# The last step of the FP4 codes on ScalarE instead of VectorE, in a transformer block with FAVOR attention

## The chip, the core and the metric

The kernel runs on one core of a Trainium2 chip. A core has a matrix engine (TensorE, PE in the profile, with its weight loads shown as PEld), a vector engine (VectorE, DVE), an engine for activation functions (ScalarE, ACT), a general engine (GpSimd, POOL) and an engine that here only issues transfers (SyncE, SP). They run at the same time and wait for one another by semaphores. Each takes its own instructions strictly in order. Operands lie in on-chip memory of 128 partitions; PE writes to a separate accumulation memory of eight banks, from which DVE and ACT read.

The metric is the device time of one execution in microseconds. A profile is one execution in which the start and end of every instruction were recorded; its span runs from the first instruction to the last.

## The reference

The input is 16 sequences of 512 rows with 256 features. One block is computed: attention with positive random features, a layer norm, a gated feed-forward network with 4-bit weights and activations, and a second layer norm.

```
q, k = softmax of 16-element heads of (x Wq + bq), (x Wk + bk)
context = (q k^T / (sum q + EPS)) v          # no softmax over rows, so k^T v is summed first
x = layernorm(x + context Wo + bo)

def fp4_quant_dequant(x):                    # along the last dimension, blocks of 16
    scale = max(max|xb| / 6, 1e-12)
    xn = xb / scale
    q = _GRID[searchsorted(_MID, |xn|)] * sign(xn) * scale

gate, up = fq(x) fq(w_gate)^T, fq(x) fq(w_up)^T      # 256 -> 704
h = silu(gate) * up
x = layernorm(x + fq(h) fq(w_down)^T)                # 704 -> 256
```

Each value is rounded to one of 0, 0.5, 1, 1.5, 2, 3, 4, 6 times the scale of its block. What matters here is how the kernel rounds.

## The kernel before

The rows are worked in 32 pairs of 128-row tiles (two pairs to a sequence). For each sequence, `project` makes q and k (line 778, evicted by DVE at 781), `features` the exponentials (ACT, 801) and their sums and reciprocals (DVE, 803 and 814, multiplied by POOL at 820), and `key_values` the summed k^T v folded with Wo (PE 836, 852, 864; ACT copies `xk` at 843 and `M` at 870). For each pair, `attend` transposes q (PE 636, ACT copy `qT` at 639), multiplies (PE 892) and does the first layer norm; the result goes to device memory and comes back later. Then the feed-forward network, pair by pair: `quantise` makes the codes of x, `gate_up` multiplies (PE 957), applies Silu (ACT 962) and the product (DVE 964) and makes the codes of h, and `down` multiplies (PE 1026) and does the second norm (`norm`, DVE 733 or, for the last two pairs, 718 to 725).

The rounding to 4 bits is done in `codes` (line 642), once for each pair over 512 elements of x and twice over 704 elements of h:

1. DVE takes the maximum of each block of 16 (655), makes the scale and its reciprocal (659, 660) and multiplies (663).
2. ACT reads the upper 16 bits of each scaled float as an integer, multiplies it by `UNTIE` and adds `MAGIC_U` = 1.5 x 2^29 (666). At that size a float has steps of 64, so the addition rounds. The result `sq` is `MAGIC_U` plus a multiple of 64.
3. DVE reads the lower 16 bits of that float and shifts them left by six (668). What it writes is the code as a 16-bit float, ready to be used as BF16: into `xc` for x, into `hcs` for h.

The codes are then transposed. DVE transposes blocks of 32 x 32 (921 for x, 1002 for h), SP writes them to device memory and reads them back regrouped (676 and 681, in `regroup`), the scales go the same way (691, 699 and 704, in `spread_scales`), and POOL multiplies codes by scales (929 for x, 1009 for h). The last pair does not take this way: DVE multiplies its codes by the scales at once (`hd`, 977), PE transposes (991), and ACT and DVE copy (995).

The weights are rounded once at the start in `fp4_exact`, which has a shift of its own (582); the change doesn't touch it.

The order of the work is made by a planner when the program is built. Every step is recorded by `op` with its engine, an assumed duration, a due time and the buffers that it reads and writes. `Plan.order` (144) then places steps one at a time: on each engine, among the steps that could start earliest, the one with the earliest due time. The instructions are issued in that order, so a change of one step's engine or assumed duration can move all others. `port=True` marks DVE steps that the planner does not place beside a POOL step. Assumed durations come from `t_act`, `t_dve`, `t_ts` and `t_pool` (250 to 263). The seven accumulation banks that PE shares among its uses are handed out by the planner too (`Share`, 78).

Of the kernel before, what the change touches and what calls it, by code (L numbers as in the profile page):

```python
# [8 lines left out]
F32 = mybir.dt.float32  # L9
# [4 lines left out]
AF = mybir.ActivationFunctionType  # L14
ALU = mybir.AluOpType
AX = mybir.AxisListType

P = 128
# [25 lines left out]
MAGIC_U = 1.5 * 2.0**29  # L44
# [51 lines left out]
class Plan:  # L96
# [7 lines left out]
    def op(self, eng, us, due, fn, ins=(), outs=(), holds=(), table=None, port=None, name=""):  # L104
        o = Op()
        o.eng, o.us, o.fn, o.due, o.table, o.name = eng, us, fn, due, table, name

        o.port = eng == "POOL" if port is None else port
        o.preds, o.succs, o.new, o.bufs, o.end = set(), [], [], [], None
        ins = [x if isinstance(x, tuple) else (x, None) for x in ins]  # L110
        outs = [x if isinstance(x, tuple) else (x, None) for x in outs]
        for b, key in ins:
            for k, w in b.last.items():
                if key is None or k is None or k == key:
                    o.preds.add(w)
        for b, key in outs:
            if b not in o.new:
                o.new.append(b)
            for k, w in b.last.items():
                if key is None or k is None or k == key:  # L120
                    o.preds.add(w)
            for k, rs in b.reads.items():
                if key is None or k is None or k == key:
                    o.preds.update(rs)
        for b, key in ins:
            b.reads.setdefault(key, []).append(o)
        for b, key in outs:
            b.last[key] = o
            b.reads[key] = []
        for b in holds:  # L130
            if b not in o.new:
                o.new.append(b)
        for b in {id(b): b for b in [b for b, _ in ins + outs] + list(holds)}.values():
            b.users += 1
            o.bufs.append(b)
        o.preds.discard(o)
        for p in o.preds:
            p.succs.append(o)
        o.left = len(o.preds)
        o.at = len(self.ops)  # L140
        self.ops.append(o)
        return o
# [107 lines left out]
def t_dve(n):  # L250
    return 0.15 + n / 960.0


def t_act(n):
    return 0.16 + n / 1200.0


def t_ts(n):
    return 0.15 + n / 1920.0
# [7 lines left out]
def tile_favor_fp4_block(  # L267
# [16 lines left out]
    nc = tc.nc  # L284
# [23 lines left out]
    const = ctx.enter_context(tc.tile_pool(name="const", bufs=1))  # L308
# [9 lines left out]
    op = plan.op  # L318
# [48 lines left out]
    def bcast(ap, n):  # L367

        return ap.unsqueeze(2).to_broadcast([ap.shape[0], ap.shape[1], n])
# [5 lines left out]
    def upper(ap):  # L375

        return ap.bitcast(U16).rearrange("p (n t) -> p n t", t=2)[:, :, 1]

    def lower(ap):

        return ap.bitcast(U16).rearrange("p (n t) -> p n t", t=2)[:, :, 0]
# [30 lines left out]
    b_o = const.tile([P, D], F32, name="b_o")  # L412
    ident = const.tile([P, P], F32, name="ident")
    neg_half = const.tile([P, 2], F32, name="neg_half")
    magic = const.tile([P, 4], F32, name="magic")

    mask = const.tile([P, P // HD, HD], F32, name="mask")
    mask2 = mask.rearrange("p g d -> p (g d)")
# [58 lines left out]
    def fill():  # L477
        make_identity(nc, ident)
        nc.gpsimd.memset(neg_half, -0.5)
        nc.gpsimd.memset(nsh, 0.0)  # L480
        nc.gpsimd.memset(hcs, 0.0)
        nc.gpsimd.memset(magic[:, 0:1], MAGIC / 2.0)
        nc.gpsimd.memset(magic[:, 1:2], -MAGIC / 2.0)
        nc.gpsimd.memset(magic[:, 2:3], MAGIC_U)
        nc.gpsimd.memset(magic[:, 3:4], 31.5 * 2.0**-65)
        nc.gpsimd.memset(mask, 1.0)
        nc.gpsimd.affine_select(
            out=mask, in_=mask, compare_op=ALU.is_ge, fill=0.0,
            base=0, pattern=[[-HD, P // HD], [0, HD]], channel_multiplier=1,
        )  # L490
        nc.gpsimd.affine_select(
            out=mask, in_=mask, compare_op=ALU.is_ge, fill=0.0,
            base=HD - 1, pattern=[[HD, P // HD], [0, HD]], channel_multiplier=-1,
        )
# [147 lines left out]
    def codes(src, xn, sq, dst, key, n, scales, at, name, due, sat=None):  # L642

        (src, src_b), (xn, xn_b), (sq, sq_b) = src, xn, sq
        amax, nscale, inv = scales
        nb = n // BLK
        g = slice(key * nb, key * nb + nb)
        gs = slice(sat, sat + nb) if sat is not None else g  # L650

        def b3(ap):
            return ap.rearrange("p (g e) -> p g e", e=BLK)

        op("DVE", t_dve(n), due, lambda: nc.vector.tensor_reduce(  # L655
            amax[:, g], b3(src()), AX.X, ALU.max, apply_absolute_value=True), ins=[src_b], outs=[(amax, key)])

        def scale():
            nc.vector.tensor_scalar(nscale[:, gs], amax[:, g], -UP / 6.0, -1e-12 * UP, ALU.mult, ALU.min)
            nc.vector.reciprocal(inv[:, g], nscale[:, gs])  # L660

        op("DVE", 0.27 + 0.0073 * nb, due, scale, ins=[(amax, key)], outs=[(nscale, key), (inv, key)])
        op("DVE", t_dve(n), due, lambda: nc.vector.scalar_tensor_tensor(  # L663
            b3(xn()), b3(src()), TIE * UP / BIG, bcast(inv[:, g], BLK), ALU.mult, ALU.mult),
           ins=[src_b, (inv, key)], outs=[xn_b], holds=[sq_b])
        op("ACT", t_act(n) + 0.14, due, lambda: nc.scalar.activation(  # L666
            sq(), upper(xn()), AF.Identity, bias=magic[:, 2:3], scale=UNTIE), ins=[xn_b], outs=[sq_b])
        op("DVE", t_ts(n), due, lambda: nc.vector.tensor_scalar(
            dst[:, at : at + n], lower(sq()), 6, None, ALU.logical_shift_left), ins=[sq_b],
           outs=[(dst, key)], port=True)  # L670

    def regroup(src, dst, n, tag, name, due):

# [233 lines left out]
    def quantise(i, due):  # L907
        x1 = st[i]["x1"] = buf([2, D], "x1", X1, f"x1_{i}")
        d = st[i]["d"]
        dma(f"rx1_{i}", 3.5, due - PAIR, lambda: nc.sync.dma_start(x1.tile, d.tile), ins=[d], outs=[x1])  # L910
        n = 2 * D
        G = n // P
        flat = lambda b: b.tile.rearrange("p u d -> p (u d)")
        am, iv = (small(n // BLK, t + "x", f"{t}_x{i}") for t in ("am", "iv"))
        scales = am, buf([n // BLK], "nsx", 2, f"ns_x{i}"), iv
        xn, sq = (buf([2, D], "xq", 2, f"{t}_{i}") for t in ("xn", "sqx"))
        xc = buf([n], "xc", 2, f"xc_{i}", U16)
        codes((lambda: flat(x1), x1), (lambda: flat(xn), xn), (lambda: flat(sq), sq), xc, 0, n, scales, 0,
              f"x{i}", due)
        xw, xcT = (buf([4, 2 * 32], t, 2, f"{t}_{i}", U32) for t in ("xw", "xcT"))  # L920
        op("DVE", 0.15 + n / 2 / 960.0, due, lambda: nc.vector.transpose(
            xw.tile.rearrange("p q (u t) -> p q u t", u=2),
            xc.tile.bitcast(U32).rearrange("p (u q t) -> p q u t", u=2, q=4)), ins=[xc], outs=[xw], port=True)
        regroup(xw, xcT, 2 * 32, "x", f"x{i}", due)
        xs_ = buf([2 * P], "xs", 2, f"xs_{i}")
        xqT = buf([2 * DC, P], "xqT", 2, f"xqT_{i}")
        spread_scales(scales[1], 1, (lambda: xs_.tile, xs_), "x", f"x{i}", due, [xqT])
        for u in range(2):
            op("POOL", t_pool(D), due, lambda u=u: nc.gpsimd.tensor_tensor(  # L929
                xqT[:, DC * u : DC * (u + 1), :].rearrange("p c (a t) -> p c a t", t=32),  # L930
                xcT.tile.bitcast(BF16).rearrange("p a (u t c) -> p u c a t", u=2, c=2)[:, u],
                xs_[:, u * P : (u + 1) * P].rearrange("p (a t) -> p a t", t=32).unsqueeze(1).to_broadcast([P, DC, 4, 32]),
                ALU.mult,
            ), ins=[xcT, xs_], outs=[(xqT, u)])
        st[i]["xqT"] = xqT
# [134 lines left out]
    with tc.manual_schedule():  # L1070
        load_all()
        fill()
        for o in plan.order():
            for b in o.new:
                b.make()
            o.fn()
# [41 lines left out]
```

## Time and profile before

| | us |
|---|---|
| median of three runs | 791.95 (791.62 to 792.87) |
| the profiled execution, its own time | 793.69 |
| its span | 792.0 |
| PE busy | 768.6 (97%) |
| DVE busy | 656.7 (83%) |
| ACT busy | 416.5 (53%) |
| POOL busy | 455.9 (58%) |
| shift, 704 elements (line 668, 64 times) | 40.0, mean 0.627 |
| shift, 512 elements (line 668, 32 times) | 18.2, mean 0.569 |
| rounding on ACT, 704 elements (line 666, 64 times) | 56.2, mean 0.878 |
| rounding on ACT, 512 elements (line 666, 32 times) | 23.1, mean 0.721 |

A row of groups reads: line, engine, operation, what it writes and reads, shape, count, busy time, mean duration of one in ns, and the idle time of the engine just before such instructions with what ended it. A matmul with 32-bit operands goes through PE in two passes, which the profile counts as two instructions. In a row of a timeline, the first number is the start in microseconds from the start of the span, the second the length; a bracket gives the idle time before and the releaser. The granted clock is the share of full speed that PE was given.

### The profile page before, as it was taken

The numbers are of one execution on the slowest core, as the hardware profiler recorded it, in microseconds if no ns is written. First come the engines' busy times: TensorE is split into PE (matmuls) and PEld (weight loads), VectorE is DVE, ScalarE is ACT, GpSimd is POOL, SyncE is SP. The second block draws the span as 40 slices with busy tenths as digits, with TensorE's granted clock in tenths as the row PEclk, the third lists the DMA queues.
The fourth block names the chain that finished last, engine by engine and source line by source line (L and its number), as shares of the span: only waits on it lengthen the run. The fifth ranks groups of instructions, "written<-read, shape, count | busy, mean of one in ns | idle before, by whom it ended". The sixth has DMA issues, their size and how long they took to land.

```text
span 792.0 us, 10915 instructions
## 1 busy us (share of the span) xinstructions
PE 768.6 (97%) x3118; PEld 552.5 (70%) x3118; DVE 656.7 (83%) x1340; ACT 416.5 (53%) x893; POOL 455.9 (58%) x602
## 2 busy tenths in 40 slices
PE   7999999989998999999999999999999999999996
PEld 3567657657676777767777777777777777777774
DVE  2998999999888798697697798888878988778784
ACT  2347766868887783544545444444334444344441
POOL 5668788889887755574554435434533543543633
PEclk9999999999999999999999999999999999999998
DMA  9112411211111044404335454554554554464441
GB/s 277 45 55 86 142 53 54 82 60 62 54 53 62 30 129 133 118 37 124 100 112 138 145 171 136 152 149 134 149 154 135 145 149 140 125 179 129 136 130 41
DMA packets 104348, 89.23 MB, mean 113 GB/s; under 512 B 44512, under 2 KB 87904, under 8 KB 104288
## 3 DMA queue, kind: packets, MB, share of 16 engines
q1 hardware_dynamic: 90704, 71.49, 31.8%
q10 hardware_dynamic: 13584, 17.04, 6.0%
q8 instruction: 25, 0.41, 0.2%
q14 instruction: 35, 0.29, 0.1%
HBM read 53.28 MB, written 35.21 MB: 112 GB/s over the span
## 4 chain that ended last, share of the span: by engine, by line
PE 62%; DVE 12%; DMA 8%; POOL 8%; issue 4%; ACT 4%; SPq 2%; ACTq 0%; POOLq 0%; DVEq 0%
PE bank L957 26%; PE bank L1026 14%; PE bank L778 8%; PE bank L892 5%; PE bank L836 5%; POOL hq L1009 3%; DMA out_dram<-y 3%; DVE qk L781 2%; PE bank L636 2%; DVE mx L786 2%; DMA hcT<-g_h 2%; SPq L681 1%; POOL xqT L929 1%; DVE fs L803 1%; PE bank L852 1%
## 5 line engine op out<-in xcount | busy, mean ns | idle before, releaser
L957 PE MATMUL bank<-w_guT,xqT 128*128 128x352 f32 x1024 | 311.3, 459 | 0.0
L957 PEld LDWEIGHTS bank<-w_guT,xqT 128*128 128x128 f32 x1024 | 193.8, 190 | 100.4 <-ACT g L962 0.2
L1009 POOL TENSOR_TENSOR hq<-hcT,hq 128x384 f32<-128x384 bf16 x124 | 127.3, 1058 | 179.3 <-DMA hcT<-g_h 101.4
L1026 PE MATMUL bank<-w_dT,hq 128*128 128x256 f32 (+1 forms) x768 | 173.1, 379 | 1.1 <-DVE r L718 1.1
L1026 PEld LDWEIGHTS bank<-w_dT,hq 128*128 128x128 f32 (+1 forms) x768 | 144.9, 190 | 27.5 <-issue 1.9
L778 PE MATMUL bank<-w_qkv,xT 128*128 128x512 f32 x256 | 120.8, 602 | 3.8 <-DVE qk L781 1.9
L964 DVE TENSOR_TENSOR h<-bank,g 128x352 f32<-128x352 f32 x128 | 65.7, 515 | 50.9 <-ACT g L962 24.1
L962 ACT ACTIVATE g<-bank 128x352 f32<-128x352 f32 x128 | 57.6, 458 | 87.7 <-PE bank L957 77.8
L666 ACT ACTIVATE sq<-h,magic 128x704 f32<-128x704 uint16 x64 | 56.2, 878 | 79.2 <-DVE h L663 78.6
L820 POOL TENSOR_TENSOR qk<-qk,fr 128x512 f32<-128x512 f32 x64 | 67.0, 1073 | 20.5 <-DVE fr L814 18.9
L790 POOL TENSOR_TENSOR qk<-qk,mx 128x512 f32<-128x512 f32 x64 | 67.4, 1068 | 19.2 <-DVE mx L786 19.0
L778 PEld LDWEIGHTS bank<-w_qkv,xT 128*128 128x128 f32 x256 | 46.6, 193 | 45.4 <-issue 35.8
L755 ACT ACTIVATE y<-r,nb_d,rstd_d 128x256 f32<-128x256 f32 x60 | 32.6, 591 | 59.2 <-POOL nb_d L748 59.2
L929 POOL TENSOR_TENSOR xqT<-xcT,xs 128x256 f32<-128x256 bf16 x64 | 46.3, 740 | 27.6 <-DMA d_h<-sT_h 23.4
L836 PE MATMUL bank<-qk,x 128*128 128x256 f32 x256 | 59.7, 387 | 2.1 <-ACT qT L639 2.1
L892 PE MATMUL bank<-M,qT 128*128 128x256 f32 x256 | 59.6, 381 | 1.8 <-ACT M L870 1.8
L655 DVE TENSOR_REDUCE bank<-h 128x44 f32<-128x704 f32 x64 | 57.1, 893 | 1.6
L663 DVE SCALAR_TENSOR_TENSOR h<-h,bank 128x704 f32<-128x704 f32 x64 | 56.7, 886 | 2.1
L836 PEld LDWEIGHTS bank<-qk,x 128*128 128x128 f32 x256 | 49.5, 195 | 12.7 <-ACT qT L639 3.4
L781 DVE TENSOR_TENSOR qk<-bank,b_qkv 128x512 f32<-128x512 f32 x64 | 43.0, 681 | 18.3 <-PE bank L778 17.9
L892 PEld LDWEIGHTS bank<-M,qT 128*128 128x128 f32 x256 | 47.8, 190 | 13.2 <-ACT M L870 3.8
L885 POOL TENSOR_TENSOR xb<-x,b_o 128x512 f32<-128x512 f32 x32 | 41.0, 1285 | 22.8 <-DVE r L733 22.7
(137 smaller groups left out, 1083.3 us busy)
## 6 DMA issues: line engine op xcount, KB each, us to landing
g_h<-hw SPq DMA_DIRECT2D x31, 384.0 KB, 2.8
hcT<-g_h SPq DMA_DIRECT2D x124, 96.0 KB, 2.4
hq<-d_h SPq DMA_DIRECT2D x31, 384.0 KB, 4.1
dx<-x1n ACTq DMA_DIRECT2D x32, 256.0 KB, 2.0
x<-dx SPq DMA_DIRECT2D x32, 256.0 KB, 3.1
x<-_attn_hidden_states_dram SPq DMA_DIRECT2D x15, 512.0 KB, 3.5
out_dram<-y ACTq DMA_DIRECT2D x30, 256.0 KB, 3.3
xs<-d_x SPq DMA_DIRECT2D x32, 128.0 KB, 2.5
```

Source lines behind the costliest of these rows:

```text
L655: op("DVE", t_dve(n), due, lambda: nc.vector.tensor_reduce(amax[:, g], b3(src()), AX.X, ALU.max, apply_absolute_value=True), ins=[src_b], ...
L778: op("PE", t_pe(D2), due, lambda c=c, u=u, pqk=pqk: nc.tensor.matmul(pqk.tile, xT[:, 2 * c + u, :], w_qkv[:, c, :D2], start=c == 0, stop=c ...
L781: op("DVE", t_dve(D2), due, lambda t=t, pqk=pqk: nc.vector.tensor_tensor(qk[:, t, :], pqk.tile, b_qkv[:, :D2], ALU.add), ins=[pqk], outs=[ ...
L790: op("POOL", t_pool(D2), due, lambda g=g: nc.gpsimd.tensor_tensor(qk3()[:, g, :], qk3()[:, g, :], bcast(mx[:, g], HD), ALU.subtract), ins= ...
L820: nc.gpsimd.tensor_tensor(f3, f3, bcast(r[:, t * 2 * H : (t + 1) * 2 * H], HD), ALU.mult)
L836: nc.tensor.matmul(pxk[:, c * D : (c + 1) * D], x[:, t, c * P : (c + 1) * P], qk[:, t, D:], start=t == 0, stop=t == TPB - 1,)
L892: nc.tensor.matmul(pu(pa.tile)[:, u, :], qT[:, 2 * u + c, :], M[:, c, :], start=c == 0, stop=c == DC - 1,)
L957: op("PE", t_pe(F2), due + u * 0.2 * PAIR, lambda c=c, u=u, lo=lo, ps_=ps_: nc.tensor.matmul(ps_[:, :F2], xqT[:, 2 * u + c, :], w_guT[:, c ...
L962: op("ACT", t_act(F2), due, lambda g=g, pg=pg: nc.scalar.activation(g.tile, pg[:, :F2], AF.Silu), ins=[pg], outs=[g], table="silu")
L964: op("DVE", t_dve(F2), due, lambda g=g, h=h, pu_=pu_, k=k: nc.vector.tensor_tensor(h[:, k * F2 : (k + 1) * F2], pu_[:, :F2], g.tile, ALU.m ...
L1009: op("POOL", t_pool(TG * P), d, lambda u=u, c=c: nc.gpsimd.tensor_tensor(hq()[:, u, :, c, :].rearrange("p g (a t) -> p g a t", t=32), hcT. ...
L1026: op("PE", t_pe(D), due, lambda f=f, g=g, c=c, n=n, u=u: nc.tensor.matmul(pu(pd.tile)[:, u, :], hq()[:n, u, g, c, :], w_dT[:n, f, :], star ...
```

## The change

The third step of `codes` goes from DVE to ACT. Instead of shifting the lower 16 bits of `sq`, ACT subtracts `MAGIC_U` from the whole float and writes the difference, a multiple of 64 below 2^16, as a 16-bit integer. These are the same 16 bits. `magic` gets a fifth column that holds -`MAGIC_U` as the bias. The planner sees an ACT step with the assumed duration of the step before it, not a DVE step with `port=True`, and makes its order anew. From line 487 on, line numbers in the changed kernel are one higher, up to the removed line; from 672 on they are the same.

```diff
-    magic = const.tile([P, 4], F32, name="magic")
+    magic = const.tile([P, 5], F32, name="magic")
...
         nc.gpsimd.memset(magic[:, 3:4], 31.5 * 2.0**-65)
+        nc.gpsimd.memset(magic[:, 4:5], -MAGIC_U)
...
         op("ACT", t_act(n) + 0.14, due, lambda: nc.scalar.activation(
             sq(), upper(xn()), AF.Identity, bias=magic[:, 2:3], scale=UNTIE), ins=[xn_b], outs=[sq_b])
-        op("DVE", t_ts(n), due, lambda: nc.vector.tensor_scalar(
-            dst[:, at : at + n], lower(sq()), 6, None, ALU.logical_shift_left), ins=[sq_b],
-           outs=[(dst, key)], port=True)
+        op("ACT", t_act(n) + 0.14, due, lambda: nc.scalar.activation(
+            dst[:, at : at + n], sq(), AF.Identity, bias=magic[:, 4:5]), ins=[sq_b], outs=[(dst, key)])
```

## The prediction

> **What bounds the kernel now.** I read the page's first two parts, then the busy time by stretches, then PE's timeline where it stood idle, and last the end of the run.
>
> ```profile
> PE 768.6 (97%) x3118; PEld 552.5 (70%) x3118; DVE 656.7 (83%) x1340; ACT 416.5 (53%) x893; POOL 455.9 (58%) x602
> PEclk9999999999999999999999999999999999999998
> ```
>
> PE is busy 97% of the span, at full clock but for small dips. In the stretches (columns: window, length, busy us of PE, PEld, DVE, ACT, POOL with counts, clock, DMA share, GB/s) PE is without a gap from 260 to 770 us; what can be won lies before and behind.
>
> ```profile
> 93.00:260.00 167.00, 159.92 (x702) 112.91 (x702) 153.43 (x276) 124.89 (x271) 139.67 (x175) 0.99 0.17 57
> 260.00:420.00 160.00, 160.00 (x665) 117.64 (x665) 128.10 (x263) 89.56 (x188) 90.30 (x119) 1.00 0.34 102
> 420.00:770.00 350.00, 350.00 (x1344) 254.41 (x1344) 289.81 (x649) 152.25 (x340) 152.89 (x214) 1.00 0.51 145
> 770.00:792.00 22.00, 14.14 (x67) 11.03 (x65) 11.74 (x30) 4.34 (x10) 8.34 (x11) 0.91 0.11 37
> ```
>
> PE's timeline names what it waited for from 100 to 260 us, and at the end (bracket: idle before, releaser). Each row is a stop:
>
> ```profile
> 105.21 0.65 PE L636 MATMUL bank<-ident,x 128*128 128x128 f32 x4 [1.04 <-DVE wxm_g L580]
> 162.87 1.13 PE L778 MATMUL bank<-w_qkv,xT 128*128 128x512 f32 x2 [0.35 <-DVE qk L781]
> 169.53 1.98 PE L778 MATMUL bank<-w_qkv,xT 128*128 128x512 f32 x4 [0.78 <-DVE qk L781]
> 173.97 1.12 PE L778 MATMUL bank<-w_qkv,xT 128*128 128x512 f32 x2 [0.68 <-ACT xT L639]
> 189.25 1.13 PE L778 MATMUL bank<-w_qkv,xT 128*128 128x512 f32 x2 [0.78 <-DVE qk L781]
> 244.08 5.41 PE L836 MATMUL bank<-qk,x 128*128 128x256 f32 x16 [2.08 <-ACT qT L639]
> ...
> 771.49 0.93 PE L991 MATMUL bank<-ident,hd 128*128 128x128 f32 x6 [0.56 <-DVE hd L977]
> 774.24 0.96 PE L991 MATMUL bank<-ident,hd 128*128 128x128 f32 x6 [0.95 <-DVE hd L977]
> 778.84 6.72 PE L1026 MATMUL bank<-w_dT,hq 128*128 128x256 f32 x30 [0.61 <-DVE r L718]
> ```
>
> In the head DVE is at 92% (153.43 of 167 us) and releases most stops; the longest is ACT's. It costs twice, since the clock falls behind it:
>
> ```profile
> 244.00:250.00 6.00, 5.92 (x21) 4.91 (x22) 4.46 (x9) 5.28 (x10) 5.62 (x7) 0.72 0.14 53
> ```
>
> At 0.72 for 6 us PE loses 6 x 0.28 = 1.7 us.
>
> **The change, part by part.** The groups of the two steps that matter:
>
> ```profile
> L666 ACT ACTIVATE sq<-h,magic 128x704 f32<-128x704 uint16 x64 | 56.2, 878 | 79.2 <-DVE h L663 78.6
> L668 DVE TENSOR_SCALAR hcs<-sq 128x704 uint16<-128x704 uint16 x64 | 40.0, 627 | 2.8 <-ACT sq L666 2.8
> ```
>
> Removed from DVE: 64 shifts of 704 at 627 ns (40.0 us) and 32 of 512 at 569 ns (18.2 us), 58 us of 656.7. Added to ACT: 64 + 32 subtractions. No row has a 16-bit output on ACT. Below stands the 512-element copy without a bias (L639 qT, 584 ns; with the slope of L666's two sizes, (878 - 721) / 192 = 0.82 ns an element, 0.74 us at 704), above L666 itself with the same bias column: 878 and 721 ns. I take L666's: 56.2 + 23.1 = 79 us, ACT to about 496 us. No DMA is added; the memset of one more column is 0.1 us at the start on POOL, which has 10.58 us of work in the first 20.
>
> [...] The rows give 627 against 878 ns, 1.4 times; if each step lay on the path, an undisturbed shift of 0.53 us against 0.878 would make 64 x 0.35 = 22 us, 814 us. The cover below is why the sum doesn't have it.
>
> Steady stretch, 260 to 770: nothing. PE's work for a pair is 32 passes of L957 in 9.47 us and 24 of L1026 in 5.18, 14.65 us. DVE's 82.8% (12.1 us a pair) falls by 2 x 0.627 + 0.569 = 1.8 to 10.3; ACT's 43.5% (6.4) rises by 2 x 0.878 + 0.721 = 2.5 to 8.9, both under 14.65. The codes reach the transposes (L1002) later: the shift at 758.15 took 0.53, the subtraction 0.88, so 0.35 us. What hides it: POOL finished that pair's hq at 762.39 and PE wanted it at 766.01, 3.6 us of slack. If that cover were gone, 0.35 x 31 pairs would be 11 us. Queued behind the subtraction on ACT are the next Silu (L962, which frees gate_up's banks), the norm and its output DMA (L1038); the transposes on DVE now wait for ACT, and behind them stand L733 and L964. ACT stood idle 77.8 us before Silu for want of PE, so those two 0.88 us have room. The changed order has the same PE sequence here, gate_up and down alternating, from about 400 us of PE work on.
>
> Head, 93 to 260 (before that the orders agree). Three terms.
> (1) DVE loses the shifts there: 0.42 + 1.00 + 0.38 + 0.42 + 0.39 + 0.52 in the 20 us windows, seven shifts, 3.1 us. Of PE's stops from 100 to 260 (the six of the fence, and 0.24 and 0.24 by ACT and 0.35 by DVE, not shown) DVE released 3.3 us and ACT 3.2: half each. Take -1.5, ends -3.1 and 0.
> (2) ACT gains about seven subtractions, six of 0.72 and one of 0.88, 5.2 us, where it is at 75% (124.89 of 167). They stand ahead of copies that free or fill PE's banks (xT, qT, xk, M). ACT is no bound by its sum, only by what stands in front; I take one or two late copies, +1.0, ends 0 and +5.2.
> (3) The order. Exp and Silu alternate on ACT at nine places before, seven after, and each table load is 1.283 us, so 2.6 us of loads go; before, two of them (231.7 and 234.8) surround a single Silu just ahead of the 2.08 us stop, and the changed order has ten Silus together there. If the stop goes, so do 2.08 + 1.7 = 3.8 us; but gate_up starts 19 us of PE work later (222 us of matmuls stand ahead of it against 203, counted in the two orders at the durations of the rows), and other stops may form. Half: -1.9; ends -3.8 and +3.8 (a like stop elsewhere).
> [...] The row shows 0.72 after a stop of 2.08. [...]
>
> Tail, from the last gate_up (PE free at 766.2). The moved step is on the chain here:
>
> ```profile
> 769.59 5.46 POOL L1009 TENSOR_TENSOR hq<-hcT,hq 128x384 f32<-128x384 bf16 x4 [5.88 <-DMA hq<-d_h]
> 770.01 1.33 DVE L977 TENSOR_TENSOR hd<-hcs,nsh 128x704 f32<-128x704 bf16 x1
> 770.12 0.88 ACT L666 ACTIVATE sq<-h,magic 128x704 f32<-128x704 uint16 x1 [3.23 <-DVE h L663]
> 771.26 1.32 DVE L668 TENSOR_SCALAR hcs<-sq 128x704 uint16<-128x704 uint16 x1
> 772.62 1.57 DVE L977 TENSOR_TENSOR hd<-hcs,nsh 128x704 f32<-128x704 bf16 x1
> ```
>
> The last shift took 1.32 us, beside POOL's stretched multiplies, and held the second L977 until 772.62. On ACT it starts at 771.0 and ends at 771.9, under the first L977. In the changed order SP issues hq<-d_h ahead of hcT<-g_h, so POOL should start about 2 us sooner; but two of pair 29's norm steps and a copy (L733, L995) now stand before the second L977, so it starts near 772.9, later than before. PE has work for that: after down(29), 5.2 us to 771.4, one matmul of pair 30 (0.43), six transposes (0.65), six more matmuls of pair 30 (2.6), so it asks for the second transposes at 775.0; L977 is ready by 774.5. The stops of 0.56 and 0.95 and the refilling behind them go, 2.0 us; of those behind L718 (0.61, 0.52) about one in two, 0.6. Take -2.5, ends -3.2 and +1.0 (the second L977 late by its 1.57).
>
> Sum: -1.5 + 1.0 - 1.9 - 2.5 = -4.9 us. The profiled execution's own time is 793.69 us (span 792.0 and 1.7 around it), 1.7 above the median of 791.95; from 793.69 it is 788.8, and from the median 787.0.
>
> **The rivals.**
> *ACT takes DVE's place in the head (slower).* Each of the seven subtractions stands ahead of a copy that PE waits for, +5.2 in place of (1) to (3), one stop passes 2 us and brings the clock down, +1.7, and the tail gives -2.5: 796.4. For it: ACT already releases the longest stop, and is at 75%; against: 42 us of idle time there. It decides once late copies pass 2.5 us, three or four of the seven. A smaller form is Silu late in the steady stretch: 0.3 us at 25 pairs, 799.5; ACT's idle time speaks against it.
> *Stops move and don't shrink.* Head as before, and the tail's gain is eaten by L733 ahead of L977: 792.0. For it: the shifts are 3 us of DVE's 153 there.
> *The head clears.* All ends below: -3.1 - 3.8 - 3.2, 781.9. Against: seven small stops in the fence are not tied to the shifts.
> That the change doesn't do its work is excluded: the 96 instructions have left DVE's order and stand in ACT's.
>
> **How the numbers follow.** Forecast 0.45, head clearing 0.12, no change 0.13, slower 0.30 (ACT in the head 0.24, Silu 0.06). A measurement of this kernel can tell about 0.2%, 1.6 us. So faster 0.57, same 0.13, slower 0.30. The range runs from 781.5 (the cleared head) to 797 (ACT in the head); outside lie the Silu case and about a tenth of the rest. The likeliest case has 784 to 790.
>
> **What would show it.** Right: DVE near 598 us, ACT near 495; subtractions at 0.72 and 0.88; PE without a gap from about 270 to 770; no stop of 2 us and no clock dip between 230 and 270; L977's stops gone before 775. Wrong: copies xT, qT, xk or M behind a subtraction as PE's releaser, more than 3 us in all; a new stop past 2 us; PE gaps before L957 released by Silu; subtractions above 0.9 us.

## The result and the profile after

The changed kernel takes 804.34 us (median of 4 runs, 803.51 to 806.49) against 791.88 for the kernel before (4 runs): ratio 1.0159, interval 1.0137 to 1.0182. It is slower by 12.5 us, outside the predicted range. Its profiled execution took 806.49 us with a span of 804.8, which is 12.8 more than the 792.0 of before. Executions whose granted clock is low throughout (one of e1 below, 0.949 and 816.85 us) are left out of every ratio, and their profiles are not read.

The page's first two parts:

```profile
PE 772.0 (96%) x3118; PEld 552.8 (69%) x3118; DVE 603.6 (75%) x1244; ACT 486.2 (60%) x987; POOL 447.4 (56%) x603
...
PEclk9999999998999999999999999999999999999999
```

Busy time moved nearly as forecast: DVE has 53 us less (58 forecast), ACT 70 more (79). The prices came as forecast, in the groups (line, engine, operation, count, busy us, mean ns):

```profile
L669 ACT ACTIVATE hcs<-sq,magic 128x704 uint16<-128x704 f32 x64 | 56.2, 879 | 1.3
...
L669 ACT ACTIVATE xc<-sqx,magic 128x512 uint16<-128x512 f32 x32 | 23.1, 722 | 0.8
```

The stretches (window, length, busy us of PE, PEld, DVE, ACT, POOL, clock, DMA share, GB/s):

```profile
93.00:260.00 167.00, 150.64 (x660) 105.63 (x659) 140.02 (x264) 120.60 (x267) 136.40 (x172) 0.98 0.18 58
260.00:420.00 160.00, 159.14 (x649) 114.50 (x648) 119.65 (x235) 103.76 (x199) 87.27 (x116) 1.00 0.32 94
420.00:770.00 350.00, 347.99 (x1338) 252.84 (x1337) 249.96 (x576) 201.47 (x405) 147.49 (x213) 1.00 0.52 144
770.00:805.00 35.00, 29.06 (x127) 22.73 (x125) 20.67 (x51) 12.52 (x27) 12.76 (x18) 0.94 0.21 68
```

In the head PE is busy 150.64 us where it was 159.92, and in the stretches that had no gap 2.9 us are now missing. To put the whole difference in its places I took, at the end of each matmul, the time minus the matmuls done so far at their undisturbed durations (0.2955 us for one of L957, 0.2158 for one of L1026, and so on). This is what PE has lost by then, to waits and to a lower clock:

| PE's loss, us | before | after | difference |
|---|---|---|---|
| up to 260 us (12.9 and 12.7 of it up to 96) | 25.5 | 37.1 | +11.6 |
| from there to the last gate_up | 0.7 | 4.6 | +3.9 |
| behind it | 3.7 | 1.0 | -2.7 |

The sum is the 12.8 us of the spans. The head's stops in PE's timeline (bracket: idle before, releaser):

```profile
131.89 3.72 PE L892 MATMUL bank<-M,qT 128*128 128x256 f32 x16 [1.11 <-ACT M L870]
139.54 3.72 PE L836 MATMUL bank<-qk,x 128*128 128x256 f32 x16 [1.33 <-DVE qk L781]
...
180.46 8.46 PE L778 MATMUL bank<-w_qkv,xT 128*128 128x512 f32 x12 [3.54 <-ACT xT L640]
...
202.82 1.13 PE L864 MATMUL bank<-w_o,kvT 128*128 128x256 f32 x4 [1.76 <-ACT xT L640]
208.50 1.99 PE L892 MATMUL bank<-M,qT 128*128 128x256 f32 x8 [0.68 <-ACT qT L640]
212.05 3.72 PE L836 MATMUL bank<-qk,x 128*128 128x256 f32 x16 [1.12 <-DVE r L733]
...
238.94 1.13 PE L778 MATMUL bank<-w_qkv,xT 128*128 128x512 f32 x2 [2.12 <-ACT M L870]
...
256.56 2.00 PE L892 MATMUL bank<-M,qT 128*128 128x256 f32 x8 [1.34 <-ACT M L870]
```

These eight waits are 13.0 us; with six shorter ones that the rows leave out, PE stops fourteen times from 100 to 260 us, for 15.7 us, where before has nine stops of 6.5 us. Behind the longest, the 12 matmuls take 8.46 us where an undisturbed group of 12 takes 5.42: 3.0 us more, by the clock (0.50 from 180 to 186 us). Most releasers are ACT's copies, which looks like the rival "ACT takes DVE's place". But what stands ahead of the late copies in ACT's queue is not the new step:

```profile
174.30 0.20 ACT L740 ACTIVATE nm_a<-rs_a 128x2 f32<-128x2 f32 x1 [3.01 <-DVE r L733]
...
175.54 0.53 ACT L566 ACTIVATE wpr_g<-bank,magic 128x352 f32<-128x352 f32 x1
176.10 0.59 ACT L567 ACTIVATE wxm_g<-wpr_g,magic 128x352 f32<-128x352 f32 x1
...
178.35 1.08 ACT L755 ACTIVATE x1n<-r,nb_a,rstd_a 128x256 f32<-128x256 f32 x2
179.45 0.33 ACTq L903 DMA_DIRECT2D dx<-x1n  x1
179.82 1.07 ACT L640 COPY xT<-bank 128x512 f32<-128x512 f32 x2 [0.40 <-ACT x1n L755]
```

PE's transposes were done at 176.9. The two copies stood behind norm steps of two pairs and the rounding of weights, and the first norm step had itself waited 3.01 us for DVE. No L669 lies between 166 and 180; the head has only three of them, at 135.0 to 165.0.

In the tail, PE's timeline has kept one stop, and both of L977 are gone:

```profile
787.16 0.85 PE L991 MATMUL bank<-ident,hd 128*128 128x128 f32 x6
...
790.44 0.85 PE L991 MATMUL bank<-ident,hd 128*128 128x128 f32 x6
...
798.01 1.56 PE L1026 MATMUL bank<-w_dT,hq 128*128 128x256 f32 x6 [0.52 <-DVE r L718]
```

### The profile page after: what moved, and what is told of

It reads as the page before. It is cut to its first block, busy times and chain, and to the rows that moved or that the text cites. A ratio compares the mean times of both kernels' runs of the same rounds, so it can differ in the third digit from the quotient of the medians.

```text
span 804.8 us, 10925 instructions
## 1 busy us (share of the span) xinstructions
PE 772.0 (96%) x3118; PEld 552.8 (69%) x3118; DVE 603.6 (75%) x1244; ACT 486.2 (60%) x987; POOL 447.4 (56%) x603
## 4 chain that ended last, share of the span: by engine, by line
PE 49%; DVE 15%; DMA 11%; POOL 10%; ACT 7%; issue 6%; SPq 2%; ACTq 1%; POOLq 0%; DVEq 0%
PE bank L957 19%; PE bank L1026 11%; PE bank L778 6%; PE bank L836 4%; PE bank L892 4%; DMA out_dram<-y 3%; POOL hq L1009 3%; DVE fs L803 2%; DMA hcT<-g_h 2%; POOL xqT L929 2%; DVE qk L781 2%; DVE ks L829 1%; DVE bank L656 1%; POOL qk L820 1%; SPq L681 1%
## 5 line engine op out<-in xcount | busy, mean ns | idle before, releaser
L957 PE MATMUL bank<-w_guT,xqT 128*128 128x352 f32 x1024 | 311.8, 459 | 2.9 <-ACT g L962 1.9
L957 PEld LDWEIGHTS bank<-w_guT,xqT 128*128 128x128 f32 x1024 | 193.8, 190 | 105.5 <-ACT g L962 3.2
L1009 POOL TENSOR_TENSOR hq<-hcT,hq 128x384 f32<-128x384 bf16 x124 | 120.7, 1006 | 218.1 <-DMA hcT<-g_h 147.9
L1026 PE MATMUL bank<-w_dT,hq 128*128 128x256 f32 (+1 forms) x768 | 172.8, 379 | 0.5 <-DVE r L718 0.5
L1026 PEld LDWEIGHTS bank<-w_dT,hq 128*128 128x128 f32 (+1 forms) x768 | 145.0, 190 | 26.4 <-issue 1.9
L778 PE MATMUL bank<-w_qkv,xT 128*128 128x512 f32 x256 | 123.2, 614 | 7.0 <-ACT xT L640 4.4
L892 PE MATMUL bank<-M,qT 128*128 128x256 f32 x256 | 60.2, 382 | 5.7 <-ACT M L870 4.3
L892 PEld LDWEIGHTS bank<-M,qT 128*128 128x128 f32 x256 | 47.9, 190 | 18.9 <-ACT M L870 6.8
L669 ACT ACTIVATE hcs<-sq,magic 128x704 uint16<-128x704 f32 x64 | 56.2, 879 | 1.3
```

The costliest lines, as they stand in the source:

```text
L778: op("PE", t_pe(D2), due, lambda c=c, u=u, pqk=pqk: nc.tensor.matmul(pqk.tile, xT[:, 2 * c + u, :], w_qkv[:, c, :D2], start=c == 0, stop=c ...
L892: nc.tensor.matmul(pu(pa.tile)[:, u, :], qT[:, 2 * u + c, :], M[:, c, :], start=c == 0, stop=c == DC - 1,)
L957: op("PE", t_pe(F2), due + u * 0.2 * PAIR, lambda c=c, u=u, lo=lo, ps_=ps_: nc.tensor.matmul(ps_[:, :F2], xqT[:, 2 * u + c, :], w_guT[:, c ...
L1009: op("POOL", t_pool(TG * P), d, lambda u=u, c=c: nc.gpsimd.tensor_tensor(hq()[:, u, :, c, :].rearrange("p g (a t) -> p g a t", t=32), hcT. ...
L1026: op("PE", t_pe(D), due, lambda f=f, g=g, c=c, n=n, u=u: nc.tensor.matmul(pu(pd.tile)[:, u, :], hq()[:n, u, g, c, :], w_dT[:n, f, :], star ...
```

## Experiments

Two theories stood against each other. **O, the order:** the planner's new order of the head costs the time, whichever engine does the step. **A, ACT's load:** the subtractions delay the copies that PE waits for. They can be separated because `op` holds two things: what the planner believes (engine, duration, `port`) and the function that issues the instruction. One can be changed without the other.

All runs at a glance; each ratio is to the kernel before, run beside it (medians 791.0 to 792.6):

| kernel | step done on | planned as | us | ratio (interval) | PE busy 93 to 260 |
|---|---|---|---|---|---|
| before | DVE | old | 791.88 | 1 | 159.92 |
| after | ACT | new | 804.34 | 1.0159 (1.0137 to 1.0182) | 150.64 |
| e1 | ACT | old | 791.53 | 0.9985 (0.9972 to 0.9999) | not read |
| e1b | ACT | old | 790.44 | 0.9989 (0.9977 to 1.0001) | 159.94 |
| e2 | DVE | new | 813.09 | 1.0253 (1.0228 to 1.0278) | 150.46 |
| p1 | DVE | old, +0.1 us | 813.77 | 1.0264 (1.0233 to 1.0295) | 148.67 |
| p2 | DVE | old, -0.05 us | 798.36 | 1.0069 (1.0037 to 1.0100) | 158.46 |
| q1 | ACT | new, +0.1 us | 802.68 | 1.0124 (1.0086 to 1.0162) | 150.63 |
| q2 | ACT | new, -0.05 us | 804.65 | 1.0148 (1.0124 to 1.0172) | 152.47 |
| h1 | ACT | new, copies moved | 804.22 | 1.0172 (1.0140 to 1.0204) | 150.11 |
| h4 | ACT | new, copies moved | 803.58 | 1.0127 (1.0105 to 1.0149) | 153.50 |
| h2 | ACT | new, copies moved | 814.56 | 1.0273 (1.0243 to 1.0303) | 149.73 |
| s1 | DVE to pair 5, then ACT | old to pair 5 | 789.77 | 0.9981 (0.9970 to 0.9993) | 159.90 |
| s2 | ACT | old to pair 5 | 788.76 | 0.9969 (0.9956 to 0.9983) | 159.87 |
| s2b | ACT | old to pair 5 | 788.60 | 0.9975 (0.9963 to 0.9986) | 159.89 |
| t4 | ACT | new to pair 5 | 805.27 | 1.0159 (1.0125 to 1.0194) | 151.65 |
| t1 | ACT | old to pair 1 | 803.50 | 1.0137 (1.0117 to 1.0157) | 151.69 |
| t5 | ACT | old to pair 9 | 794.99 | 1.0030 (1.0017 to 1.0043) | 159.92 |
| t3 | ACT | old to pair 27 | 791.28 | 0.9983 (0.9969 to 0.9997) | 159.84 |
| s3 | ACT | old to pair 5, a copy moved | 789.81 | 0.9983 (0.9971 to 0.9995) | 159.86 |

### The step without the order, the order without the step

e1 does the subtraction on ACT, recorded as the old DVE shift, so that the order stays that of before; e2 the reverse.

```diff
 # e1 (against after)
-        op("ACT", t_act(n) + 0.14, due, lambda: nc.scalar.activation(
-            dst[:, at : at + n], sq(), AF.Identity, bias=magic[:, 4:5]), ins=[sq_b], outs=[(dst, key)])
+        op("DVE", t_ts(n), due, lambda: nc.scalar.activation(
+            dst[:, at : at + n], sq(), AF.Identity, bias=magic[:, 4:5]), ins=[sq_b],
+           outs=[(dst, key)], port=True)
 # e2 (against after)
-        op("ACT", t_act(n) + 0.14, due, lambda: nc.scalar.activation(
-            dst[:, at : at + n], sq(), AF.Identity, bias=magic[:, 4:5]), ins=[sq_b], outs=[(dst, key)])
+        op("ACT", t_act(n) + 0.14, due, lambda: nc.vector.tensor_scalar(
+            dst[:, at : at + n], lower(sq()), 6, None, ALU.logical_shift_left), ins=[sq_b], outs=[(dst, key)])
```

> The subtraction on ACT, but planned as if it were the old shift on DVE, so that all instructions stand in the order of before and only the 96 steps change their engine. Theory O (the new order makes the loss; the step itself costs little): PE's stops in 93 to 260 us come back to those of before, about 7 us of idle time there, and the whole run is 790 to 795 us. Theory A (the subtractions delay what ACT does for PE): the head keeps some 16 us of idle PE time and the run is 800 us or more.

> The shift on DVE again, but planned as the subtraction on ACT, so that all instructions stand in the order of the changed kernel. Theory O: the head keeps its stops, some 16 us of idle PE time in 93 to 260 us; the run is 799 to 806 us. Theory A: the head's stops on ACT go and the run is 795 us or less. In both, the stops before L957 by Silu at 720 and 737 us go (2 us), since ACT has no subtractions there.

Measured: 0.9985 and 1.0253. e1b is e1 once more, beside s1 and s2 of below, and its profile is the one read here:

> The kernel with the order of before and the subtraction on ACT once more, for its profile: 790 to 793 us. Theory O: some 7 us of idle PE in 93 to 260 us as before, PE without a gap from 270 to 770. The subtractions stand where the shifts stood, so Silu may come late: up to 2 us of stops before L957.

PE's head in e1b, first the stretch and then the end of it:

```profile
93.00:260.00 167.00, 159.94 (x707) 113.05 (x706) 151.26 (x272) 127.78 (x275) 140.37 (x175) 0.99 0.16 57
```

```profile
242.83 5.41 PE L837 MATMUL bank<-qk,x 128*128 128x256 f32 x16 [2.09 <-ACT qT L640]
```

It is the head of before, down to the stop of 2.09 us at 242.83 (before 2.08 at 244.08). The four subtractions that ACT has in this stretch (three of 512 elements, one of 704) changed nothing in it, in either direction. In e2, with the shift on DVE, PE stops where it does in after, by the same releasers:

```profile
181.02 7.11 PE L778 MATMUL bank<-w_qkv,xT 128*128 128x512 f32 x12 [3.55 <-ACT xT L640]
```

For the head theory A falls, O stands. e2 came out well above the 799 to 806 us expected: the long stops for Silu at 720 and 737 are gone, as expected (0.26 us is the longest left), but at this order DVE, with the shifts back, is late in the steady stretch (L733 releases PE after up to 1.83 us), and PE is busy 343.84 of the 350 us from 420 to 770, against 347.99. So at the new order the new step is even the better one: e2 is 8.7 us slower than after.

### Other new orders, without the change

p1 and p2 leave every instruction of before, q1 and q2 every one of after. Only the duration that the planner assumes for the step differs, which is enough to make the order anew.

```diff
 # p1, p2 (against before)
-        op("DVE", t_ts(n), due, lambda: nc.vector.tensor_scalar(
+        op("DVE", t_ts(n) + 0.1, due, lambda: nc.vector.tensor_scalar(
...
+        op("DVE", t_ts(n) - 0.05, due, lambda: nc.vector.tensor_scalar(
 # q1, q2 (against after)
-        op("ACT", t_act(n) + 0.14, due, lambda: nc.scalar.activation(
+        op("ACT", t_act(n) + 0.24, due, lambda: nc.scalar.activation(
...
+        op("ACT", t_act(n) + 0.09, due, lambda: nc.scalar.activation(
```

> The kernel before, with the shift on DVE; only the duration that the planner assumes for it is 0.1 us longer, which makes it plan anew. Theory O in its strong form (any new order of the head moves the time by several us, up or down): a time more than 3 us from 791.9, by stops in 93 to 260 us. Theory A and the weak form (the order of the change is bad because ACT is fuller in it): within 2 us of 791.9.

> The changed kernel; only the duration that the planner assumes for the subtraction is 0.1 us longer. Theory O, strong form: the head's stops come elsewhere and the time moves by more than 3 us from 804.3, to somewhere from 790 to 808. Theory A: 802 to 807, with stops on ACT in the head as before.

> The kernel before, its instructions unchanged, with the planner's assumed duration of the shift 0.05 us shorter. If the order before was a lucky one among its neighbours, any new order loses in the head: 800 to 815. If the 22 us that a longer assumed shift cost came from its direction (the shift believed longer, its work put later), a shorter one leaves 790 to 794.

> The kernel after, its instructions unchanged, with the planner's assumed duration of the subtraction 0.05 us shorter. If the order is what costs, the time is anywhere between 790 and 815, with stops in the head at other places than after (not 180.46 by xT and 238.94 by M). If the subtractions themselves cost, the time is 803 to 806 and the stops have a copy behind a subtraction as releaser.

Measured: +2.6%, +1.2%, +0.7%, +1.5%. p1, the kernel before with one assumed number changed, loses more than the change did, with other stops in the head:

```profile
149.68 3.78 PE L778 MATMUL bank<-w_qkv,xT 128*128 128x512 f32 x4 [3.90 <-DVE wdn L534]
...
175.44 0.75 PE L852 MATMUL bank<-xk,w_qkv 128*128 128x128 f32 x4 [4.28 <-ACT xk L843]
192.40 0.63 PE L636 MATMUL bank<-ident,qk 128*128 128x128 f32 x4 [3.35 <-DVE wpr_g L582]
```

q1, at 802.68 us, moved by less than the 3 us that the strong form of O asked for and lies where A had it; but its stops are others, the longest 5.76 us at 128.81. p2 came out below what I expected of O (798.4 against 800 to 815), with its loss at other places too: 1.23 and 2.52 us at 220 to 223 and 2.30 by `hd` in the tail. q2 did not differ as O had it: its stops are those of after, 3.54 us at 179.88 and 2.13 at 237.02, although the plan was made anew. So not every change of a number moves the head, but of the four that were tried none came out as good as the order of before.

### Single places in ACT's queue

Is one bad place the cause? h4 takes after's order and issues the two copies of the 3.54 us stop directly behind their transposes. h2 does so with every xT and qT. (h1 was meant to be h4 but names the copies of the sequence before; its stop stayed, 3.56 us at 180.13, so it says nothing on the place.)

```diff
-        for o in plan.order():
+        order = plan.order()
+        for o in [o for o in order if o.eng == "ACT"]:
+            of = [p for p in o.preds if p.eng == "PE" and p.name in ("xT_10_0", "xT_10_1")]
+            if of and len(o.bufs) == 2:
+                order.remove(o)
+                order.insert(order.index(of[0]) + 1, o)
+        for o in order:
```

> The changed kernel with one thing moved in its order: the two ACT copies xT that PE waited 3.54 us for at 180.46 us stand directly behind their transposes, ahead of the norm, its output DMA and three weight steps. Theory O (the place in ACT's queue makes the stop): the stop and the 0.4 us a matmul lost to the lower clock behind it go, up to 7 us, of which DVE, late there too, gives back some: 797 to 802 us. If ACT is late for its sum of work (theory A): another stop takes its place and it stays at 803 to 806.

> The order after the change, but the two copies xT that PE awaits in its longest stop (3.54 us at 180.46, pair 5) are issued on ACT directly behind their transposes, ahead of the norm and weight steps. If the place of these two copies in ACT's queue makes the stop, it goes, and with it the clock loss behind it: 804.3 - 3.5 - 2 to 3 = about 798, and no stop above 2.2 us between 170 and 200 us. If the other engines are simply short of time in that stretch, a stop of like size forms within the next 30 us, behind the norm or weight step that now comes later, and the time stays at 803 to 805.

> The order after the change, but every copy xT and qT on ACT is issued directly behind its transposes. If places in ACT's queue make the head's stops, those released by xT and qT (3.54, 1.76 and 0.68 us) go, with the clock loss of 2 to 3 us: 804.3 - 6 - 2.5 = about 796. If the copies now wait at the front of the queue and hold up the other ACT work, stops released by M, xk and DVE grow by as much: 803 or more.

In h4 the stop falls from 3.54 to 0.24 us and the 12 matmuls take 5.42 again, 6.3 us won on the spot. Most of it is gone soon after:

```profile
178.05 5.42 PE L778 MATMUL bank<-w_qkv,xT 128*128 128x512 f32 x12 [0.24 <-ACT xT L640]
184.79 0.44 PE L637 MATMUL bank<-ident,qk 128*128 128x128 f32 x2 [1.33 <-POOL qk L820]
185.81 0.44 PE L637 MATMUL bank<-ident,qk 128*128 128x128 f32 x2 [0.58 <-POOL qk L820]
...
237.51 2.06 PE L778 MATMUL bank<-w_qkv,xT 128*128 128x512 f32 x2 [2.12 <-ACT M L870]
```

PE now waits for POOL's features, and the stop by `M` ends 1.4 us earlier than in after (237.51 against 238.94). Half speed now follows at two places. The clock is 0.86 from 182 to 188 us and 0.85 from 188 to 194, which is 1.7 us short; at 237.51 two matmuls and the eight behind them take 2.06 and 2.69 us, in after 1.13 and 1.89, again 1.7 us: as much as the 3.4 us lost to the clock behind after's stop. The span gains 2.4 us, the median 0.8 (by the ratios 0.3%, within their intervals). The place of the copies made that stop, but the other engines were nearly as late: most of the loss is the order's, not one place's. In h2 the sum of the stops grew, 814.56 us: what the copies no longer wait for now waits for them (`M` 3.42 us at 244.16 and 2.98 at 261.86).

### Which steps bring the order that loses

The step is done on ACT everywhere (s1 excepted), and the planner is told the old or the new one by the pair. s2 plans pairs 0 to 5 as the shift of before and the rest as the change does; s1 is s2 with the shift itself back on DVE for these pairs; t4 is the mirror of s2; t1, t5 and t3 switch at pair 2, 10 and 28.

```diff
+        i = int(name[1:].split("_")[0])
+        subtract = lambda: nc.scalar.activation(
+            dst[:, at : at + n], sq(), AF.Identity, bias=magic[:, 4:5])
+        if i < 6:       # t4: i > 5; t1: i < 2; t5: i < 10; t3: i < 28
+            op("DVE", t_ts(n), due, subtract, ins=[sq_b], outs=[(dst, key)], port=True)
+        else:
+            op("ACT", t_act(n) + 0.14, due, subtract, ins=[sq_b], outs=[(dst, key)])
```

> The same order as the split with all subtractions on ACT, but pairs 0 to 5 keep the shift on DVE itself. Beside that run it gives the price of 18 subtractions in the head at a fixed order. Theory O: within 1.5 us of it, either way. Theory A: at least 4 us faster than it.

> The subtraction on ACT for all pairs; the planner still takes it for the old shift on DVE in pairs 0 to 5, whose codes are made in the head, and as the subtraction on ACT from pair 6 on. Theory O: the head has the order of before and loses no more than it, and the end keeps the order of the changed kernel, which lost 2.7 us less than before from 770 us on; with 4 us lost by late Silu as in the changed kernel it is 792 to 794, without that loss 788 to 790. Theory A: 797 or more.

> The subtraction on ACT everywhere; planned as an ACT step for pairs 0 to 5 alone, from pair 6 on as the old shift. If the order that these first pairs bring makes the loss, the time is 800 to 810 and PE loses 8 us or more more than before between 93 and 260 us. If the loss needs the later steps' plan too, the time is 789 to 793.

> The subtraction on ACT everywhere; planned as the old shift for pairs 0 and 1 alone, as an ACT step from pair 2 on. If any other plan of steps that fall into the head spoils its order, 797 to 815. If only the first two pairs' steps matter, 788 to 791.

> The subtraction on ACT everywhere; planned as the old shift for pairs 0 to 9, as an ACT step from pair 10 on. If only the head's order and the tail's matter, it is as the switch at pair 6: 787.5 to 789.5. If the steady stretch loses or wins by the order too, it differs from that by more than 1.5 us.

> The subtraction on ACT everywhere; planned as the old shift for pairs 0 to 27, as an ACT step from pair 28 on. If the tail's gain belongs to the last pairs alone, PE's stops before the last transposes go and the time is 790.4 - 2.5 = about 788. If it comes from an order that begins earlier, the tail's stops stay and the time is 790 to 791.

With e1b and after, s2 and t4 make a square: new plan nowhere 790.44, from pair 6 on 788.76, up to pair 5 only 805.27, everywhere 804.34. The plan of the first six pairs carries the whole loss; what it changes is the order and, with it, which banks the planner hands out, and no run here parts these two. t4 has after's stop, too (its line numbers behind 675 are 7 higher than after's, those of s2, s3, t1, t3 and t5 too; e1b's are 1 higher):

```profile
180.02 7.11 PE L785 MATMUL bank<-w_qkv,xT 128*128 128x512 f32 x12 [3.54 <-ACT xT L640]
```

t1, with only two pairs left as they were, loses as much with a different stop, 7.30 us at 181.01. s1 and s2 have one order and differ only in the engine for the first six pairs; their intervals overlap.

t5 was expected to be as s2 if the steady stretch were neutral. It is not: 1.0030 against 0.9969. Its head is that of before; the difference is in the steady stretch, where PE stops three times for Silu (0.53, 0.79 and 1.10 us, 2.4 in all), and, in its profiled execution, in the clock behind the stop at 243 (1.7 us, below). After has the same kind. This is ACT ahead of such a stop in after:

```profile
731.51 0.88 ACT L667 ACTIVATE sq<-h,magic 128x704 f32<-128x704 uint16 x1 [2.90 <-DVE h L664]
732.42 0.88 ACT L669 ACTIVATE hcs<-sq,magic 128x704 uint16<-128x704 f32 x1
733.21 0.71 ACT L667 ACTIVATE sqx<-xn,magic 128x512 f32<-128x512 uint16 x1
733.95 0.72 ACT L669 ACTIVATE xc<-sqx,magic 128x512 uint16<-128x512 f32 x1
...
735.80 0.79 ACT L962 ACTIVATE g<-bank 128x352 f32<-128x352 f32 x2
```

PE's answer to it:

```profile
736.29 1.45 PE L957 MATMUL bank<-w_guT,xqT 128*128 128x352 f32 x4 [1.31 <-ACT g L962]
```

Here the subtractions do stand ahead of what PE waits for. It is the one place where theory A has something, and only in some orders: e1b, s2 and t4 are busy for 349.86, 350.00 and 350.00 of these 350 us.

t3 asked whether the tail's gain belongs to the last two pairs' plan. Its stop by `hd` is 1.47 us, and at 0.9983 it is not faster than e1b; in e1b both stops by `hd` are gone at the old order. So the step alone is enough for that part of the tail's gain. But the order alone is enough, too. In e2 the shift is on DVE again and takes as long as before, and PE's two groups of transposes have no stop:

```profile
793.94 1.32 DVE L669 TENSOR_SCALAR hcs<-sq 128x704 uint16<-128x704 uint16 x1
```

```profile
794.56 0.85 PE L991 MATMUL bank<-ident,hd 128*128 128x128 f32 x6
...
797.84 0.85 PE L991 MATMUL bank<-ident,hd 128*128 128x128 f32 x6
```

Counted as in the table of PE's loss, e2 loses 1.0 us behind the last gate_up, as after does, and e1b 2.1 (before 3.7).

### The better kernel, and one more place

s2 beats both kernels, and s2b repeats it. s3 is s2 with the copy qT of its 2.09 us stop issued directly behind its transposes, by the same few lines as h4 with `qT_22`.

> The kernel that plans pairs 0 to 5 as before and the rest with the subtraction, once more, beside the one with the copy moved: 788 to 789.5, and faster than the kernel before by 2 to 4 us.

> The kernel that plans pairs 0 to 5 as before and the rest with the subtraction (788.8 us), with one copy qT, which PE awaits for 2.09 us at 242.67, issued on ACT directly behind its transposes, ahead of two norm steps and two weight steps. If a place in ACT's queue can be won where the other engines are not late, the stop goes and the time is 788.8 - 2.1 = about 786.7. If the gain only moves on, as it did in the changed kernel's order, the time is 788 to 789 and a stop of 1 to 2 us forms within 30 us.

s2b: 788.60 us, ratio 0.9975 (0.9963 to 0.9986), 2.4 us better than before. s3: 789.81, not better. The stop went and others came 5 us later:

```profile
245.47 0.66 PE L637 MATMUL bank<-ident,qk 128*128 128x128 f32 x4 [1.60 <-DVE wpr_d L583]
246.68 3.00 PE L785 MATMUL bank<-w_qkv,xT 128*128 128x512 f32 x4 [0.56 <-ACT g L969]
```

The 3.00 us for four matmuls, 1.98 elsewhere, show that half speed follows (the clock is 0.72 from 245 to 251 us), which s2b does not have behind its stop of 2.09 (1.00 there). Even in the good order a freed place passes the wait on, here to DVE's weight step and to Silu. Differences of 1 us among s1, s2, s2b and s3 should not be read further: s2b's eleven runs lie at 788.2 to 788.6 us (six, mean clock 0.999) or at 789.3 to 790.1 (five, 0.996 or 0.997), about as far apart as one such stretch of half speed costs (1.7 us).

## Why the prediction was wrong, by its steps

- **What bounds the kernel: right.** The time moved with PE's stops in the head, not with DVE's or ACT's sums.
- **The prices: right.** 0.722 and 0.879 us against L666's 0.721 and 0.878. The sums were a little off: DVE 603.6 (598 forecast), ACT 486.2 (496).
- **Head, terms (1) and (2), DVE's relief and ACT's late copies, -1.5 and +1.0: near in the sum, each too large.** At the old order (e1b) PE's head is 159.94 against 159.92 us, at the new one (after against e2) 150.64 against 150.46. The two do not trade gains: both are about nothing. The count of seven was a misreading: three of the seven shifts (0.42 and 1.00 us in the rows) lie ahead of 93 us. The head has four, 1.7 us, and four subtractions on ACT would be 3.0 us, not 5.2.
- **Head, term (3), the order: the step that failed.** It had -1.9 with ends at ±3.8; it measured +11.6 us. I counted what could leave (one stop and its clock loss) and took "a like stop elsewhere" as the worst. What the runs show instead is a whole order exchanged: fourteen stops of 15.7 us in all and a clock loss of 3.4 us in place of before's nine stops of 6.5 us and a clock loss of 1.7; the instructions in the old order (e1b) have none of the difference. The sign was drawn from one stop that I could see, while the order of before was itself the better part of what was to be lost. The mark that was there to be read is PE's 159.92 of 167 us: with so little left to win and so much to lose, a new order's ends are not alike. The prediction's own upper ends (0, +5.2, +3.8 and +1.0) add up to 802 us, above the 797 at which its range stopped.
- **Steady stretch, nothing: wrong by 3.9 us.** The sums per pair (8.9 us on ACT against 14.65 on PE) hold, but four roundings and subtractions in one row, as at 731.5, make Silu late. It was named as a small rival at 0.3 us in 25 pairs; it came as two waits of 0.64 and 1.31 us, beside 0.86 us by DVE's `h` at 352. Each of the three cost PE about 0.27 us more than its idle time (two matmuls of L957 start 1.47 us late at the 1.31, the next 0.10), and a short one at 733 brought 0.3. The mean hid it: ACT's 77.8 us of idle time before Silu do not help where its steps stand in a row.
- **Tail, -2.5: right in size,** -2.7, with the work that the new order gives PE between the transposes as forecast. But taking the last shift off DVE, from which the part began, was not needed for it: with the shift on DVE at the new order (e2) the tail is the same, and the step alone (e1b) gave 1.6.
- **Rival "ACT takes DVE's place" (796.4): the wrong mechanism** with the right sign. The releasers look like it; e1b, with the same subtractions on ACT, has none of it, and e2, without them, has the same stops.
- **What would show it wrong** was named rightly (a new stop past 2 us; xT and M as releasers; gaps before L957 by Silu), but "behind a subtraction" was not found in the head.

Had every step lain on the path, the move would have come to 814 us by the rows. At an unchanged order it costs nothing (e1b 0.9989), and at the new order it is worth 8.7 us against the shift (e2). The slower step (0.879 against 0.627 us) was not on the path.

What stays open: which decision among the first pairs' steps turns the planner to the worse order, whether the order of the instructions or the banks handed out with it make the stops, and whether orders better than that of before can be had by more than the 0.3% of s2.

## What to carry to other kernels

Where a greedy planner makes the order, a moved step is two changes, the step and a new order, and they should be priced and measured apart: record the step as the old one to keep the order, then let the plan change stretch by stretch. A head that is nearly full is more easily lost than won by a new order (seven new plans of it, with the step or without, were 0.7 to 2.6% slower; three of them, after, q2 and t4, have the same stops, so that five different ones were seen), so the range must reach further on that side. A releaser names the last wait, not the cause: twice a stop was taken away at its releaser (h4, s3), and within 10 us another engine had taken its place.

## What the runs showed of the hardware

The granted clock fell to 0.50 behind some of PE's stops and stayed at 1.00 behind others. Before's row by row, in single microseconds (the clock is the third number from the end):

```profile
244.00:245.00 1.00, 0.92 (x4) 0.84 (x5) 1.00 (x2) 1.00 (x3) 1.00 (x2) 1.00 0.14 53
245.00:246.00 1.00, 1.00 (x4) 0.80 (x4) 0.54 (x2) 0.43 (x2) 1.00 (x2) 0.57 0.00 0
246.00:247.00 1.00, 1.00 (x4) 0.82 (x3) 0.83 (x2) 0.98 (x2) 0.62 (x2) 0.50 0.51 201
247.00:248.00 1.00, 1.00 (x4) 0.73 (x4) 0.18 (x2) 0.99 (x3) 1.00 (x2) 0.50 0.16 62
248.00:249.00 1.00, 1.00 (x5) 0.86 (x4) 0.97 (x2) 0.95 (x2) 1.00 (x2) 0.72 0.00 0
249.00:250.00 1.00, 1.00 (x8) 0.86 (x7) 0.93 (x3) 0.93 (x2) 1.00 (x2) 1.00 0.00 0
```

The four shortfalls are 1.7 us, half speed for 3.4 us, and this is the 0.72 of the six-microsecond row. After's is 0.90 at 179, 0.50 from 180 to 186, 0.69 at 186: 3.4 us of shortfall, half speed for 6.8, twice as long.

But the same stop does not always bring it. Behind a stop of 2.08 or 2.09 us the same 16 matmuls took 5.41 us in before, e1b and t5 (the clock is 0.72 from 243 to 249 us; in s1, too) and 3.72 in s2, s2b and t3 (1.00 there). Behind the stop by `M`, 2.12 us in h4 and after and 2.13 in q2, h4 lost 1.7 us as said above; in q2 the eight matmuls of L892 and the two behind them took 3.21 and 1.44 us, where after has 1.89 and 1.02, again 1.7 us. Behind the stop of about 3.54 us the 12 took 7.11 us in t4 and e2 and 7.12 in q2, 1.7 more than the undisturbed 5.42, and 8.46 in after, 3.0 more. So the length of a stop alone did not tell what it cost in the clock; what decided it is left open here.

A stop of about 2 us then cost 0 or 1.7 us in the clock, and 1.7 us is more than the step itself was worth here (e1b 0.9989, 0.9 us).
